# When the value operands' differences are made in the queries' sweep of a transformer block

## The chip, the cores and the metric

The kernel runs on one core of a Trainium2 chip. A core has a matrix engine (TensorE, PE), a vector engine (VectorE, DVE), a scalar engine (ScalarE, ACT), a general engine (GpSimd, POOL), and a queue that issues transfers (SyncE, SP). Each of them works through its own list of instructions in order, and they wait for each other by semaphores. SBUF is the on-chip memory; PSUM holds matrix results. The metric is the time of one execution on the device in microseconds (us), smaller being better.

## The reference

One pre-norm transformer block in float32, on x of 2048 tokens by 1024 features. The attention is among the 32 heads of one token, not among tokens; the feed-forward weights are first rounded to a table of 16 values (NF4) in blocks of 64.

```
h = layernorm(x)
q, k, v = h @ wq.T + bq, h @ wk.T + bk, h @ wv.T + bv      # as (token, 32 heads, 32)
scores = einsum('bshd,bstd->bsht', q, k) / sqrt(32)
x = x + einsum('bsht,bstd->bshd', softmax(scores), v)
h = layernorm(x)
gate, up = h @ dq1.T, h @ dq2.T                            # dq = nf4(w), 2752 wide
x = x + (silu(gate) * up) @ dq3.T
```

## The kernel before, in words

**Three sweeps and the feed-forward.** The queries', the keys' and the values' projections are three sweeps over the tokens, each in eight iterations of one pair of 128-token tiles (`NP` = 8). Then come the two feed-forward products. Every projection of a pair is a 2 x 2 block product by Strassen's scheme in Winograd's form: seven products instead of eight. `products` (L373) runs them; each product is eight matmuls on PE of 128 x 128 by 512 (`mm4`, four instructions of the program, two passes each in the trace), into the PSUM tiles z, q, r and y. ACT copies intermediate sums out of PSUM (g0, s7, u2, u4) and DVE adds the results to ce and co. After the second product and after each one behind it `products` calls `fill(n)`, where the caller puts other work: n = 7, 6, 2, 5, 3 and 4 in this order.

**The operands of a pair.** The seven products need the four quarters of the normed, transposed tokens, A11, A12, A21, A22, and four sums and differences of them, S1 to S4. The class `Inputs` (L501) makes them in the queries' sweep for all three sweeps:
- `normed_x` (L496) norms both x tiles into xn: statistics and the final step on DVE, the inverse deviation rs on POOL.
- `transposes(j)` (L513) transposes xn tile j on PE, four quarters into one PSUM tile pt, two pt per call. ACT copies each pt twice: into the operands A of the queries and keys (L520), and with the columns in another order into the operands V of the values (L522). The quarter A21 goes to tiles of its own, A21 and V21.
- `finished` (L528) lets DVE make the four differences of A (L420, L421, L422, L425), and stores A to opD of the pair in DRAM for the keys' sweep.
- `finished_v` (L532) does the same four for V and stores it to opV for the values' sweep.

pt has three buffers (`ps_t`, L475). A has two. V (tag AV), A21 and V21 have one buffer each, so a new pair's copy into AV waits until the differences of the pair before are made and its store to opV has landed.

**One iteration p of the queries' sweep** (L597): the loads of the next two x tiles are issued and their norms written down; the seven products of pair p run; at `fill(5)`, between the fifth and the sixth product, PE transposes pair p+1. After the products come the differences of A of pair p+1 (`nxt.finished`), the transposes of the queries' result and their stores to qD (`qk_T`), then `now.finished_v`, the differences of V of pair p, and a chunk of the differences of the weights of the keys or values (`weight_chunk`, L575: DVE steps at L582 to L585, loads cB, stores wtD).

**The background.** The feed-forward weights are rounded to the table by a generator, `background` (L242): per 128 x 1024 tile some fifteen steps, each one DVE operation (L257, L259, L261, L267) and mostly one ACT operation ahead of it (L266), and scalings in sixteen small ACT operations (L218). `advance` lets it go on a step at a time, `flush` transposes a finished weight tile.

**What sets the order.** PE's order is as written. The orders of DVE, ACT, POOL and SP are set when the program is built, by a scheduler that takes the written order as priority and places an instruction when, by its own estimate, what it needs is there. `tc.issue_after(x)` makes what is issued inside stand behind instruction x; `opened` is the last of the first weights' differences. So the place of a call in the text is not yet its place in an engine's list: in the program built, V's differences of pair p (called behind the products of iteration p) begin before pair p+1's copies into AV, since these need the buffer.

Of the kernel before, what the change touches and what calls it, by code (L numbers as in the profile page):

```python
# [69 lines left out]
def preln_block_kernel(  # L70
# [133 lines left out]
    def flush(steps=3):  # L204
        for _ in range(steps):
            if pending and next(pending[0], flush) is flush:
                pending.pop(0)
# [72 lines left out]
    def advance(n):  # L280
        for _ in range(n):
            with turn():
                next(bg, None)
# [78 lines left out]
    def mm4(dst, w, xop, start, stop):  # L362
        for k in range(4):
# [7 lines left out]
            )  # L371

    def products(A, fill, used=lambda name: None, apart=None):  # L373

        def mul(dst, a, w, start, stop):
            mm4(dst, A[:, a], W[w], start, stop)
            used(w)

        def copied(nm, src):
            t = pair.tile([P, TB], FP, tag=nm, name=nm)
            marked(nc.scalar.copy(t, src))  # L383
            return t

        z = ps_pj.tile([P, TB], FP, tag="z", name="z")
        mul(z, SA11, "B11", True, False)
        g0 = copied("g0", z)
        q = ps_pj.tile([P, TB], FP, tag="q", name="q")
        mul(q, S3, "T3", True, False)  # L390
        s7 = copied("s7", q)
        fill(7)
        mul(z, S2, "T2", False, False)
        u2 = copied("u2", z)
        fill(6)
        r = bank("r")
        mul(r, SA12, "B21", True, True)
        ce = pair.tile([P, E], FP, tag="C0", name="ce")
        co = pair.tile([P, E], FP, tag="C1", name="co")
        nc.vector.tensor_tensor(ce[:, 0:512], g0, r, ALU.add)  # L400
        fill(2)
        mul(z, S1, "T1", False, apart is not None)
        u4 = copied("u4", z)
        nc.vector.tensor_tensor(co[:, 512:], u4, s7, ALU.add)
        fill(5)
        if apart is None:
            mul(z, S4, "B22", False, True)
            marked(nc.scalar.copy(ce[:, 512:], z))
        else:
            y = apart.tile([P, TB], FP, tag="y", name="y", bufs=1)  # L410
            mul(y, S4, "B22", True, True)
            nc.vector.tensor_tensor(ce[:, 512:], u4, y, ALU.add)
        fill(3)
        mul(q, SA22, "T4", False, True)
        nc.vector.tensor_tensor(co[:, 0:512], u2, q, ALU.add)
        fill(4)
        return ce, co
# [14 lines left out]
    def qk_T(t, c, b):  # L432

        nc.vector.transpose(t, c.rearrange("p (h d) -> p h d", d=D))
        nc.vector.tensor_tensor(t, t, b.unsqueeze(2).to_broadcast([P, 32, 32]), ALU.add)
# [43 lines left out]
    def load_x(i):  # L479
        xt[i] = work.tile([P, E], FP, tag="x", name="xt", bufs=2)  # L480
        for n in range(2 if i == 0 else 1):
            cols = ts(n, TB) if i == 0 else slice(None)
            load = nc.sync.dma_start(xt[i][:, cols], xf[ts(i, P), cols])
        if i == 2:
            tc.add_manual_dep(
                load.ins,
                opening["first"].name,
                mybir.DependencyInfo(
                    mybir.DependencyClass.Sync, mybir.DependencyReason.DATA
                ),  # L490
                reason="the first weights come first",
            )
# [53 lines left out]
    nxt = Inputs(0)  # L546
# [25 lines left out]
    opened = last.ins  # L572
    nc.sync.dma_start(opD[0], nxt.A)

    def weight_chunk(m, k):  # L575

        b = {}
        for nm in ("B11", "B12", "B21", "B22"):
            b[nm] = work.tile([P, TB], FP, tag=f"c{nm}", name=f"c{nm}")
            nc.sync.dma_start(b[nm], block(m, int(nm[1]) - 1, int(nm[2]) - 1)[:, k, :])  # L580
        t3 = work.tile([P, TB], FP, tag="cT3", name="cT3")
        nc.vector.tensor_tensor(t3, b["B22"], b["B12"], ALU.subtract)  # L582
        nc.vector.tensor_tensor(b["B12"], b["B12"], b["B11"], ALU.subtract)
        nc.vector.tensor_tensor(b["B22"], b["B22"], b["B12"], ALU.subtract)
        nc.vector.tensor_tensor(b["B21"], b["B21"], b["B22"], ALU.subtract)  # L585
        for n, t in ((1, b["B12"]), (2, b["B22"]), (3, t3), (4, b["B21"])):
            nc.sync.dma_start(wtD[m, n][:, k, :], t)

    def next_W(m):
        return lambda name: load_W(m, name)  # L590

    def load_A(src, p):
        t = pair.tile([P, 7, 4, P], FP, tag="A", name="A", bufs=2)
        nc.sync.dma_start(t, src[p])
        return t

    for p in range(NP):  # L597
        more = p + 1 < NP
        now = nxt
        urgent["rule"] = ("scale",) if p == 0 else ()  # L600
        if more:
            load_x(2 * p + 2)
            load_x(2 * p + 3)
            with nullcontext() if p else tc.issue_after(opened):
                nxt = Inputs(p + 1)
            if p == 0:
                with tc.issue_after(hook["normed"]):
                    nc.vector.tensor_tensor(W["T4"], W["B21"], W["T2"], ALU.subtract)

        def fill(n):  # L610
            if n in (7, 3):
                flush(1)
            if n == 5 and more:
                nxt.transposes(0)
                nxt.transposes(1)
            with nullcontext() if p else tc.issue_after(opened):
                advance({3: 3, 4: 2}.get(n, 0) if p == 0 else int(n != 5))

        cs = products(now.A, fill, (lambda name: None) if more else next_W("k"), ps_t)
        flush(1)  # L620
        if more:
            nxt.finished()
        for j in range(2):
            t = work.tile([P, 32, NH], FP, tag="qd", name="qd", bufs=2)
            qk_T(t, cs[j], qb_sb)
            nc.sync.dma_start(qD[2 * p + j], t)
        with nullcontext() if p else tc.issue_after(opened):
            now.finished_v()
        weight_chunk("kv"[p // 4], p % 4)
        advance(2)  # L630
        if p == NP - 2:
            first = load_A(opD, 0)
# [553 lines left out]
    now = Unit(*units.pop(0))  # L1186
    now.first()
    for n, (g, tbp) in enumerate(passes):
        half, sides = None, []
        while now is not None and now.tbp == tbp and now.c in g:  # L1190
# [6 lines left out]
            if g[-1] == NFULL and unit.c == NFULL - 1:  # L1197
# [5 lines left out]
                now = None  # L1203
            if units:
                now = Unit(*units.pop(0))
# [52 lines left out]
```

## Time and profile before

| | us |
|---|---|
| median of 3 runs | 2465.94 (2464.23 to 2466.81) |
| profiled execution | 2468.05 |
| its span | 2466.28 |
| PE busy | 2384.2 (97% of the span) |
| DVE busy | 2015.7 (82%) |
| ACT busy | 1514.9 (61%) |
| POOL busy | 290.0 (12%) |
| mean clock granted to PE | 0.989 |

How to read the profile's lines that follow further down. A line of the waits names the waiting engine and tile, what ended the wait, and the total time, the number of waits and the longest one. A line in order of time has start, duration, engine, source line, operation, tiles written and read, and in square brackets the idle time ahead of it and what ended it. A line of stretches has the stretch, its length, the busy time of PE, of PE's weight loads, DVE, ACT and POOL with the number of instructions, then PE's granted clock (1 is full speed), the share of the transfer engines and GB/s. L numbers are lines of the kernel.

### The profile page before, as it was taken

Reading aid. Unit: us, or ns where it says so; the run is one execution under the profiler, and the core shown is the slowest. Engines: PE = TensorE matmul, PEld = TensorE weight load, DVE = VectorE, ACT = ScalarE, POOL = GpSimd, SP = SyncE. Lnnn points to the kernel's source line nnn. Section 1 sums busy time; section 2 is a strip of 40 time slices with the busy share of each in tenths; the row PEclk is TensorE's granted clock in tenths of the full one; section 3 lists DMA queues with packets and bytes.
Section 4 is the critical chain, followed back from the end, with each engine's and each line's share of the span. In section 5 each row is a group of like instructions: output and inputs, shape, how many; then the busy total and the mean of one; then the engine's idle time right before and its main releaser. Section 6 shows DMA issues by size and latency. Waiting matters only on the chain.

```text
span 2466.3 us, 36345 instructions
## 1 busy us (share of the span) xinstructions
PE 2384.2 (97%) x14000; PEld 1114.6 (45%) x14000; DVE 2015.7 (82%) x2239; ACT 1514.9 (61%) x2819; POOL 290.0 (12%) x364
## 2 busy tenths in 40 slices
PE   8899999999998899999999999999999999999998
PEld 4444455545554344444444444444444444444433
DVE  8999888679899789898989989899898998861022
ACT  4556644134445678778787786977878778751200
POOL 1010000001001012030030301203012030020300
PEclk9999999999998999999999999999999999999999
DMA  8788643656779577485784858848588385772983
GB/s 320 279 298 351 237 161 115 230 204 224 231 247 317 192 261 164 141 177 187 280 178 141 177 172 298 171 147 182 163 294 194 125 187 160 276 167 78 179 317 113
DMA packets 179549, 513.87 MB, mean 208 GB/s; under 512 B 15984, under 2 KB 70256, under 8 KB 156976
## 3 DMA queue, kind: packets, MB, share of 16 engines
q1 hardware_dynamic: 138672, 438.08, 48.7%
q0 software_dynamic: 40704, 73.47, 18.2%
q8 instruction: 110, 1.80, 0.3%
q14 instruction: 63, 0.52, 0.1%
HBM read 283.69 MB, written 227.80 MB: 207 GB/s over the span
## 4 chain that ended last, share of the span: by engine, by line
DVE 23%; issue 21%; PE 14%; ACT 7%; DMA 3%; POOL 1%; DVEq 0%; POOLq 0%; ACTq 0%; SPq 0%
DVE r L267 15%; PE z L364 5%; DMA x1d<-acc 3%; PE z L1070 2%; ACT sg L266 2%; PE q L364 2%; ACT wn L218 2%; PE po L1151 1%; ACT r L218 1%; PE y L1070 1%; DVE r L259 1%; DVE r L261 1%; ACT acc L1083 1%; DVE am L230 1%; PE rr L364 1%
## 5 line engine op out<-in xcount | busy, mean ns | idle before, releaser
L267 DVE SCALAR_TENSOR_TENSOR r<-sg,r 128x1024 f32<-128x1024 f32 x780 | 946.8, 1214 | 84.8 <-ACT sg L266 51.6
L266 ACT ACTIVATE sg<-wn 128x1024 f32<-128x1024 f32 x780 | 815.1, 1054 | 305.9 <-DVE r L267 280.6
L1085 POOL DMA_DIRECT2D x1d<-acc x280 | 244.2, 926 | 1281.0 <-ACT acc L1083 1238.1
L364 PE MATMUL z<-xB,w 128*128 128x512 f32 x720 | 327.1, 602 | 5.9 <-ACT u L989 4.2
L364 PE MATMUL z<-xT,w 128*128 128x512 f32 x656 | 300.5, 601 | 11.7 <-ACT g L975 8.0
L364 PE MATMUL q<-xT,w 128*128 128x512 f32 x656 | 291.3, 592 | 0.0
L1070 PE MATMUL z<-w,h 128*128 128x512 f32 x496 | 230.8, 593 | 2.9 <-ACT acc L1083 2.9
L364 PEld LDWEIGHTS z<-xB,w 128*128 128x128 f32 x720 | 135.1, 193 | 170.2 <-issue 152.9
L364 PEld LDWEIGHTS z<-xT,w 128*128 128x128 f32 x656 | 123.2, 192 | 165.7 <-issue 139.5
L218 ACT ACTIVATE wn<-wn,rc 128x64 f32<-128x64 f32 x736 | 189.3, 341 | 8.9 <-DVE rc L238 8.9
L364 PEld LDWEIGHTS q<-xT,w 128*128 128x128 f32 x656 | 123.2, 190 | 148.6 <-issue 146.4
L364 PE MATMUL z<-wT,A 128*128 128x512 f32 x384 | 177.1, 604 | 0.1
L364 PE MATMUL q<-wT,A 128*128 128x512 f32 x384 | 172.8, 592 | 0.0
L1070 PE MATMUL y<-w,h 128*128 128x512 f32 x320 | 152.0, 596 | 3.6 <-DVE h L1048 3.1
L364 PE MATMUL z<-wB,A 128*128 128x512 f32 x320 | 148.5, 608 | 2.0 <-ACT u L383 2.0
L364 PE MATMUL rr<-xB,w 128*128 128x512 f32 x328 | 147.5, 592 | 0.0
L1070 PEld LDWEIGHTS z<-w,h 128*128 128x128 f32 x496 | 92.6, 190 | 116.9 <-issue 100.8
L218 ACT ACTIVATE r<-r,am 128x64 f32<-128x64 f32 x456 | 116.6, 344 | 16.1 <-DVE r L267 16.0
L1083 ACT COPY acc<-z 128x512 f32<-128x512 f32 x160 | 92.6, 585 | 38.0 <-PE z L1070 29.7
L364 PEld LDWEIGHTS q<-wT,A 128*128 128x128 f32 x384 | 72.1, 190 | 86.7 <-issue 84.9
L985 DVE TENSOR_TENSOR g<-g,rr 128x512 f32<-128x512 f32 x41 | 28.0, 682 | 100.7 <-PE rr L364 100.7
L137 POOL TENSOR_TENSOR rs<-mv,eps 128x1 f32<-128x1 f32 x32 | 18.0, 562 | 762.5 <-DVE mv L134 762.5
(136 smaller groups left out, 2733.6 us busy)
## 6 DMA issues: line engine op xcount, KB each, us to landing
x1d<-acc POOLq DMA_DIRECT2D x280, 256.0 KB, 6.5
wd<-wop SPq DMA_DIRECT2D x31, 2048.0 KB, 7.3
w<-wd SPq DMA_DIRECT2D x41, 1280.0 KB, 7.7
wn<-in_w_dram SPq DMA_DIRECT2D x63, 512.0 KB, 4.2
xT<-xdT SPq DMA_DIRECT2D x28, 1024.0 KB, 8.5
xB<-xdB SPq DMA_DIRECT2D x24, 1024.0 KB, 7.0
w<-wd SPq DMA_DIRECT2D x42, 512.0 KB, 4.4
w<-wd SPq DMA_DIRECT2D x10, 1536.0 KB, 7.6
```

What stands on the lines that cost most here:

```text
L218: nc.scalar.mul(dst[:, ts(n, BLOCK)], src[:, ts(n, BLOCK)], by[:, n : n + 1])
L230: nc.vector.tensor_reduce(am[:, :nb], v.rearrange("p (b e) -> p b e", e=BLOCK), AX.X, ALU.max, apply_absolute_value=True,)
L259: nc.vector.scalar_tensor_tensor(r, v, edge, r, ALU.is_lt, ALU.max)
L261: nc.vector.scalar_tensor_tensor(r, v, edge, r, ALU.is_gt, ALU.subtract)
L266: nc.scalar.activation(t, v, AF.Copy, bias=-edge * by, scale=by)
L267: nc.vector.scalar_tensor_tensor(r, t, code, r, ALU.min, ALU.max)
L364: nc.tensor.matmul(dst, w[:, k, :], xop[:, k, :], start=start and k == 0, stop=stop and k == 3, skip_group_check=True,)
L985: nc.vector.tensor_tensor(self.g0, self.g0, r, ALU.add)
L1070: nc.tensor.matmul(dst, side[n][:, ts(q, P)], w3T[g[2 * m]][:, W3[n]], start=start and m == 0, stop=stop and m == 1, skip_group_check=True,)
L1083: nc.scalar.copy(t, src)
L1085: nc.gpsimd.dma_start(x1d[8 * tbp + 2 * q + j][n], t, accum_op=ALU.add)
L1151: nc.tensor.matmul(po, hs[c][j][:, ts(q, P)], w3T[c][:, ts(n, 512)], start=(c == g[0]), stop=False, skip_group_check=True,)
```

## The change

V's differences and their store are called one iteration earlier: directly behind `nxt.finished()`, for pair p+1 in iteration p, where before they were called for pair p in iteration p, behind the queries' results. Pair 0, whose transposes stand ahead of the loop, gets its differences of V in iteration 0 at `fill(7)`, behind `opened` as before.

```diff
         def fill(n):
             if n in (7, 3):
                 flush(1)
+            if n == 7 and p == 0:
+                with tc.issue_after(opened):
+                    now.finished_v()
             if n == 5 and more:
                 nxt.transposes(0)
                 nxt.transposes(1)
...
         flush(1)
         if more:
             nxt.finished()
+            nxt.finished_v()
         for j in range(2):
             t = work.tile([P, 32, NH], FP, tag="qd", name="qd", bufs=2)
             qk_T(t, cs[j], qb_sb)
             nc.sync.dma_start(qD[2 * p + j], t)
-        with nullcontext() if p else tc.issue_after(opened):
-            now.finished_v()
         weight_chunk("kv"[p // 4], p % 4)
```

## The prediction

> **What bounds the kernel now.** I read the totals first, then the stretches, then in the queries' sweep the waits and the order of time on TensorE (PE), ScalarE (ACT) and VectorE (DVE). "0.60 apart" below means start to start; listed durations overlap a little.
>
> From the page, the stretches and the waits of the first 240 us:
>
> ```profile
> PE 2384.2 (97%) x14000; PEld 1114.6 (45%) x14000; DVE 2015.7 (82%) x2239; ACT 1514.9 (61%) x2819; POOL 290.0 (12%) x364
> ...
> 0.00:240.00 240.00, 218.57 (x606) 105.87 (x607) 221.73 (x301) 126.74 (x268) 24.64 (x52) 0.96 0.82 309
> 240.00:480.00 240.00, 235.83 (x3659) 124.03 (x3657) 193.64 (x197) 108.09 (x216) 0.00 (x0) 1.00 0.48 181
> 720.00:860.00 140.00, 120.12 (x1563) 61.25 (x1562) 119.35 (x133) 79.91 (x167) 7.92 (x12) 0.91 0.74 247
> ...
> PE pt L517 <- ACT V L522: 13.0, 7, 2.4
> PE pt L517 <- DVE xn L358: 6.9, 3, 3.1
> ```
>
> PE bounds the whole, but not the queries' sweep (to 243 us): there DVE is the busier, 221.7 of 240 us. PE's own losses there are the two waits, both at the transposes, and the clock.
>
> Order of time, PE in iterations 3 and 4 of the sweep, ACT in iteration 4, and DVE in iteration 3:
>
> ```profile
> 118.32 1.04 PE L517 MATMUL pt<-ident,xn 128*128 128x128 f32 x8
> 121.43 0.79 PE L517 MATMUL pt<-ident,xn 128*128 128x128 f32 x4 [2.07 <-DVE xn L358]
> 123.39 1.12 PE L517 MATMUL pt<-ident,xn 128*128 128x128 f32 x4 [1.17 <-ACT V L522]
> 124.30 5.76 PE L364 MATMUL y<-wB,A 128*128 128x512 f32 x8
> ...
> 150.50 1.47 PE L517 MATMUL pt<-ident,xn 128*128 128x128 f32 x12
> 154.36 0.66 PE L517 MATMUL pt<-ident,xn 128*128 128x128 f32 x4 [2.39 <-ACT V L522]
> 154.85 3.60 PE L364 MATMUL y<-wB,A 128*128 128x512 f32 x8
> ...
> 152.25 1.57 ACT L520 COPY A<-pt 128x512 f32<-128x512 f32 x3
> 153.69 0.62 ACT L522 COPY V<-pt 128x512 f32<-128x512 f32 x1
> 157.47 1.53 ACT L522 COPY AV<-pt 128x512 f32<-128x512 f32 x3
> ...
> 120.56 0.81 DVE L358 TENSOR_SCALAR xn<-xt,mv,rs 128x1024 f32<-128x1024 f32 x1 [0.71 <-POOL rs L138]
> ```
>
> There are three pt buffers. The fourth transpose group needs one back. AV has one buffer too, still held by the pair before, so ACT first makes three A copies and the V21 copy, which frees the third pt: with u4 ahead, five copies 0.48 apart. That gives a 1.33 us stall at best (iterations 0 and 5) and 2.06 to 2.39 where u4 itself started 0.7 to 1.1 late behind other ACT work. In iteration 3 the second xn is late.
>
> The clock is the other loss:
>
> ```profile
> 63.00:69.00 6.00, 6.00 (x14) 2.74 (x14) 4.74 (x7) 4.90 (x14) 0.00 (x0) 0.72 0.00 0
> 124.00:130.00 6.00, 6.00 (x12) 2.70 (x11) 3.87 (x7) 3.21 (x6) 0.00 (x0) 0.61 0.62 226
> ```
>
> After the 2.06 us gap of iteration 1 and the two gaps of iteration 3 the y and q behind them ran at 0.72 and 0.61: y took 5.13 and 5.60 us to the next product instead of 3.43, so 1.7 and 2.2 lost. Gaps of 2.28 to 2.39 in iterations 2, 4 and 6 lost nothing.
>
> **The change, part by part.**
>
> 1. *Instructions.* None is added or removed: per set, four subtractions and additions of 0.60 (2.4 us DVE), and one opV store, eight sets. PE's order and POOL's are the same in the built program. ACT's, DVE's and SP's change up to the first pair of the keys' sweep; from there all are as before.
>
> 2. *Iteration 0.* The built order still copies A, A, A21, V21, A and only then AV three times, behind opV0. Gain 0; the 1.33 stays. On DVE, AV's first subtraction takes the slot of a 1.1 us reduction ahead of xn, so DVE idles 0.48 until rs.
>
> 3. *Iterations 1 to 6, ACT.* AV is free a pair earlier, so the order is A, AV, A, AV, A21, V21, A, AV. The fourth group now waits for the first AV copy, the third copy instead of the fifth: 2 x 0.48 = 0.96 less, 0.37 where u4 is on time. New wait: that AV copy for the previous opV to land, with the other copies and PE's fourth group behind it. Landing took 5.7 to 12.4 us (median 7.3); from issue to need there are at least 12 (iteration 1), elsewhere 15 or more. So 0; at the longest 12.4, some 0.3 once.
>
> 4. *SP.* opV moves from among the loads to directly behind opD, past both qD stores (pair 1's past one). It waits for DVE's last AV operation; the qD behind it waits for a later DVE addition anyway. So nothing behind, the x and weight loads included, starts later through it. 0, bounds 0 to 0.4 (an issue, 0.33).
>
> 5. *DVE, the cover.* Each set used to spread over its iteration. Now V of pair p+1 is done before the next pair's second xn, which gates PE. Counting the built orders up to the second xn of iterations 2 and 3: the set stands 2.4 us earlier in 2; at 3 the sets are even but one 1.14 step, the 1.1 reduction and 0.85 of small rows have moved ahead, 3.1 more. As check, the sum of my start-to-start rows over before's order from xn to xn is 69.6 us plus 3.95 idle, against 73.53 in the trace.
>
> Laid out with those rows (PE's transposes due / second xn done / y starts; before in brackets):
> - it. 1: 60.16 / 60.16 / 61.6 [63.32]. Gap 0.4, so y keeps full clock: next product 3.4 earlier.
> - it. 2: 86.5 / 87.5 / 89.9 [93.41]. xn costs 1.0; ACT's u4 stands behind a step that waits for DVE, 1.4 more. Gain kept at 3.5, none added.
> - it. 3: 115.7 / 121.5. DVE reaches this xn at 120.7 (before 120.56), whatever PE does: a 5.8 us gap. The copies' wait of 1.17 is gone, y starts at 123.2 [124.30] at half clock until the next window ends (125.2 on before's grid), and the next product comes at 127.7 [129.90]: 2.2 earlier. One more half-clock window leaves 0.5. **The 3.5 us of iterations 1 and 2 are lost here.**
> - it. 4: xn in time; u4 behind sixteen small ACT scalings to 149.05; y 151.15 [154.85], 3.7 earlier.
> - it. 5: stall 0.5 for 1.33; y 177.9 [182.62], 4.7 earlier.
> - it. 6: DVE again. The second x tile's load stands on SP behind a wtD store that waits for DVE to 174.4; loads landed in 2.6 to 8.3 us, median 5.7, so 180.5 where DVE wants it at 179.1: 1.3 lost (0 to 4). Then step, ACT step, u4, A, AV: y at 206.25 without that loss, 207.5 with it [211.35], 5.1 or 3.9 earlier. The gap is 2.0 to 3.3 us; a half-clock window costs 1.7. Gaps over 2 us in the trace cost it in two iterations of five; the longer gap I give 0.65, the shorter 0.4: 3.9 - 0.65 x 1.7 = 2.8 with the load late, 5.1 - 0.4 x 1.7 = 4.4 with it on time.
>
> I take the middle of these, **3.5 us** earlier at the end of the sweep; the ends are 2.3 later (load at its latest and two windows, rival C) and 5.1 earlier.
>
> 6. *Behind the sweep* every order is the same, PE is busy 235.8 of 240, and DVE has 46 us idle, so I carry the shift to the end. Cover gone: the windows of 720 to 860 ran at 0.91, 0.18 x 140 = 25 us of half clock; gaps falling otherwise in the windows could give or take one or two of 1.7 us.
>
> Of the clock the Trainium skill (TensorE: Matmul & The Clock Gate, "HAM oscillation — how this bites in real kernels") says that PE should have no idle gap above about 3.4 us. The trace tripped at 2.06. By the page's rule the gap of iteration 6 is free and the sum would be 4 to 5 us; with the trace's it is 3.5.
>
> **The sum and its base.** The profiled execution took 2468.05 (span 2466.28, 1.8 around it), 2.1 above the median of the runs, 2465.94. Off both: profile 2464.5, median **2462.4**. A measurement here tells about 0.2%, 4.9 us, from no change.
>
> **The rivals.**
> - *B, full gain.* DVE is no bound and all seven stalls shrink: 6 x 0.96, the late u4 (0.73 + 1.1 + 1.1 + 0.95 = 3.9), xn's 2.07 and the clock's 3.9 are 15.6 at most; DVE's idle time of 18.3 in 240 us, of which some 10 is the opening, allows about 8. For: small idle gaps of 0.4 to 0.7 at rs. Against: xn of iteration 3. Time 2458; 2456 to 2461.
> - *C, slower.* The x load of iteration 6 at its longest: 8.3 us lands at 183.1, DVE 4 late, y at 210.3 after a gap of 6 us, two half-clock windows 3.4: 2.3 later than before, 2468.3. The load may take 4.3 before DVE waits; above 6.0, with two windows, the sign turns (5.1 = 1.7 + 3.4). For: one of the seventeen took 8.3, the median is 5.7. Against: the trace of before has waits for x only at the start.
> - *D, all absorbed.* Second half-clock window in iteration 3 and one in 6, or DVE's lag handed to the keys' sweep: 2465 to 2467. For: xn of iteration 3 comes at the same time in both orders. Against: iterations 4 and 5 have DVE to spare (xn 8 us early).
> - *The change does nothing* is true of iteration 0 alone; ACT's copies do change from 1 on.
>
> **How the numbers follow.** Forecast 0.53, B 0.20, C 0.10, D 0.17. Faster by over 0.2% (below 2461.0): B at 0.18 and the forecast's tail 0.13, 0.31. Slower by over 0.2% (above 2470.9): most of C's high part, where the later windows fall badly too, 0.09. Within: 0.60. The forecast's own range is 2460.5 to 2464.5. The range for all, 2457.0 to 2467.5, leaves out B's low end and C's upper half.
>
> **What would show it.** Right: in iterations 1 to 6 ACT goes A, AV, A, AV, and "pt waits for ACT V" is replaced by waits for AV, with iteration 1 and 5 at 0.4 to 0.5 us; in iteration 3 a PE gap of 5 to 6 us that ends at xn near 121.5 us, and low clock behind it; the sweep's last product ends 2 to 5 us before 242.3; the rest shifts as one. Wrong: a second xn of iteration 3 well before 120 us (then B); a DVE wait for x in iteration 6 of over 2 us or a longer sweep (C); a keys' sweep whose PE waits have grown (D).

## The result, and the profile after

The changed kernel takes 2477.93 us (median of 5 runs, 2473.82 to 2478.33) beside 2465.59 for the kernel before: 1.0043 times as long, 95% interval 1.0031 to 1.0054. It is slower by 12.3 us between the medians and by 10.6 by the ratio, where 3.5 us of gain was forecast; the measurement lies outside the range on record, 2457.0 to 2467.5. Two of the five runs took 2473.8 and 2473.9 and three 2477.9 to 2478.3; the profiled execution, 2478.13 (span 2476.3), is one of the three.

The same stretches as before, of the changed kernel (columns: stretch, length, busy time of PE, PE's weight loads, DVE, ACT and POOL, PE's clock, share of the transfer engines, GB/s):

```profile
0.00:240.00 240.00, 217.69 (x594) 105.69 (x595) 218.44 (x295) 127.11 (x273) 23.24 (x52) 0.96 0.81 303
240.00:480.00 240.00, 231.15 (x3521) 121.28 (x3520) 192.79 (x199) 104.20 (x208) 0.00 (x0) 0.98 0.46 171
```

The queries' sweep is about as busy as before (217.7 of 240 us of PE for 218.6). The loss shows in the second row: 4.7 us less PE, at a clock of 0.98 for 1.00. PE's waits in these 480 us:

```profile
PE pt L517 <- DVE xn L358: 13.4, 5, 6.5
PE pt L517 <- ACT AV L522: 5.8, 4, 3.5
PE sc L450 <- DMA ql<-qD: 4.9, 1, 4.9
...
PE pt L517 <- ACT V L522: 1.3, 1, 1.3
```

The waits for V have gone from 13.0 us to 1.3, as forecast, and those for AV are 5.8. But the waits for xn have doubled, from 6.9 to 13.4 (some 5 of either are the opening, ahead of the sweep's iterations), and there is a new one: the scores (`sc`, the first of the keys' sweep) wait for `ql`, a load of the stored queries. In order of time on PE, iterations 3 and 6 of the queries' sweep and the place of the new wait:

```profile
117.70 1.04 PE L517 MATMUL pt<-ident,xn 128*128 128x128 f32 x8
125.22 1.97 PE L517 MATMUL pt<-ident,xn 128*128 128x128 f32 x8 [6.48 <-DVE xn L358]
...
206.94 1.47 PE L517 MATMUL pt<-ident,xn 128*128 128x128 f32 x12
211.93 1.12 PE L517 MATMUL pt<-ident,xn 128*128 128x128 f32 x4 [3.51 <-ACT AV L522]
212.83 6.10 PE L364 MATMUL y<-wB,A 128*128 128x512 f32 x8
...
285.11 1.79 PE L450 MATMUL sc<-kd,ql 32*32 32x32 f32 x128 [4.94 <-DMA ql<-qD]
286.83 5.03 PE L364 MATMUL z<-wT,A 128*128 128x512 f32 x8
```

Before, the same two instructions of the keys' sweep ran without a gap and at full clock:

```profile
276.37 1.77 PE L450 MATMUL sc<-kd,ql 32*32 32x32 f32 x128
278.07 3.70 PE L364 MATMUL z<-wT,A 128*128 128x512 f32 x8
```

So 4.94 us of wait and 5.03 - 3.70 = 1.33 of half clock arise at one place. What `ql` stood behind is seen on SP, first before, then after:

```profile
249.99 2.05 SPq L587 DMA_DIRECT2D wtDv<-cB  x2
252.09 1.24 SPq L587 DMA_DIRECT2D wtDv<-cT  x1
253.37 1.27 SPq L587 DMA_DIRECT2D wtDv<-cB  x1
254.68 1.25 SPq L594 DMA_DIRECT2D A<-opD  x1
257.81 0.84 SPq L691 DMA_DIRECT2D ql<-qD  x2
```

```profile
249.81 3.18 SPq L630 DMA_DIRECT2D qD<-qd  x2
253.04 1.18 SPq L580 DMA_DIRECT2D cB<-in_wvT_dram  x2
254.28 0.80 SPq L594 DMA_DIRECT2D A<-opD  x1
272.37 0.33 SPq L587 DMA_DIRECT2D wtDv<-cB  x1
272.75 0.42 SPq L587 DMA_DIRECT2D wtDv<-cT  x1
274.11 1.52 SPq L587 DMA_DIRECT2D wtDv<-cB  x2
275.72 0.38 SPq L594 DMA_DIRECT2D A<-opD  x1
276.16 1.59 SPq L693 DMA_DIRECT2D ql<-qD  x3
```

Two loads of the last weight chunk (`cB`, in fact cB21 and cB22) stand in the changed program behind the seven loads of the keys' weights, which wait for PE, and behind the last two stores to qD. They are issued at 253.04. So DVE makes the chunk's steps L582 to L585 among the keys' sweep's own work, where the kernel before had finished them in the queries' sweep. The last step before, then the first and the last after:

```profile
229.21 0.69 DVE L585 TENSOR_TENSOR cB<-cB,cB 128x512 f32<-128x512 f32 x1
```

```profile
269.93 0.69 DVE L582 TENSOR_TENSOR cT<-cB,cB 128x512 f32<-128x512 f32 x1
...
274.60 0.68 DVE L585 TENSOR_TENSOR cB<-cB,cB 128x512 f32<-128x512 f32 x1
```

The four wtDv stores wait for DVE on SP (17.2 us ahead of the first), and the `ql` loads behind them are issued at 276.16 where they were issued at 257.81. Not all of this is the transfer: these transfers landed at most 7.3 us after their issue, so the two loads were there by 261.3, and DVE, without a gap, came to the first step 8.6 us later. The place of the steps in DVE's list adds to the place of the loads in SP's.

How far each point of PE's list of products is behind the kernel before, from the starts of the same product in the two profiled executions (us; the runs are introduced below; the time given is that of the kernel before):

| kernel | 229: behind the last transposes | 266: keys, pair 0 | 296: behind the first scores | 432 | end |
|---|---|---|---|---|---|
| changed | +4.0 | +3.7 | +10.1 | +11.8 | +10.0 |
| a1_pool | +2.5 | +2.2 | +8.7 | +10.2 | +7.9 |
| a8_load2 | +1.7 | +1.2 | +1.2 | +2.8 | +1.6 |
| b1_late | +1.4 | +1.4 | +11.0 | +12.4 | +6.9 |
| b8_load2 | +1.7 | +1.4 | +1.4 | +1.3 | +0.5 |
| b3_move | -8.1 | -10.0 | -5.6 | +0.4 | -3.7 |
| a3n_move | -2.4 | -3.4 | -2.3 | +3.4 | +5.7 |
| c16_even | -5.8 | +0.8 | +8.6 | +8.8 | +8.6 |

Of the changed kernel's first +4.0, 1.1 are there before any changed instruction runs (the first x landed later in that execution). A gap of two microseconds costs half clock in one execution and not in another, too (behind the 2.06 us gap of iteration 1, y lost 1.7 us in the kernel before and nothing in b8_load2): single profiles of one order differ by 1 to 2 us at the end of the sweep.

### The profile page after: what moved, and what is told of

It is laid out like the page before. It is cut to its first block, busy times and chain, and to the rows that moved or that the text cites. A ratio compares the mean times of both kernels' runs of the same rounds, so it can differ in the third digit from the quotient of the medians.

```text
span 2476.3 us, 36360 instructions
## 1 busy us (share of the span) xinstructions
PE 2389.1 (96%) x14000; PEld 1117.4 (45%) x14000; DVE 2016.6 (81%) x2239; ACT 1511.3 (61%) x2819; POOL 288.5 (12%) x364
## 4 chain that ended last, share of the span: by engine, by line
DVE 28%; issue 18%; PE 12%; ACT 7%; DMA 2%; POOL 1%; DVEq 0%; POOLq 0%; ACTq 0%; SPq 0%
DVE r L267 18%; PE z L364 5%; ACT sg L266 2%; DMA x1d<-acc 2%; ACT wn L218 2%; PE q L364 2%; ACT r L218 1%; PE z L1072 1%; DVE r L259 1%; DVE r L261 1%; PE po L1153 1%; DVE am L230 1%; ACT acc L1085 1%; PE rr L364 1%; PE po L1164 1%
## 5 line engine op out<-in xcount | busy, mean ns | idle before, releaser
L267 DVE SCALAR_TENSOR_TENSOR r<-sg,r 128x1024 f32<-128x1024 f32 x780 | 946.5, 1214 | 83.1 <-ACT sg L266 47.5
L137 POOL TENSOR_TENSOR rs<-mv,eps 128x1 f32<-128x1 f32 x32 | 17.5, 546 | 776.0 <-DVE mv L134 759.3
```

The costliest lines, as they stand in the source:

```text
L267: nc.vector.scalar_tensor_tensor(r, t, code, r, ALU.min, ALU.max)
```

## The experiments

Theory 1: the late chunk and what it does to SP make the loss. Theory 2: the queries' sweep has lost the time itself, through DVE (late xn) or ACT, and the wait for ql only takes slack. Times are compared as ratios to the kernel before on the same chip.

**a1_pool: the stores off SP.**

```diff
-            nc.sync.dma_start(wtD[m, n][:, k, :], t)
+            (nc.gpsimd if (m, k) == ("v", 3) else nc.sync).dma_start(wtD[m, n][:, k, :], t)
```

> The changed kernel, with one edit: the four stores wtDv of the last weight chunk are issued on POOL's queue and not on SP's. The orders of PE and DVE stay the same. On SP the loads of ql, which stood behind these stores, come right behind the load of opD of the second pair. Theory 1 (SP's queue): the wait of PE's first scores for ql (4.94 us) and the half clock behind it (z 5.03 instead of 3.70 us, 1.33) go, and nothing takes their place: 6.3 us off 2477.9, so 2471.6, bounds 2469 to 2473.5; in the trace no PE wait for ql, and PE's first scores some 2 to 4 us later than in the kernel before (276.4) instead of 8.7. Theory 2 (the queries' sweep has lost the time, and the ql wait only took slack that a later wait takes as well): within 2 us of the changed kernel, 2476 to 2480, with another wait of about 5 us in the keys' sweep.

Measured 2474.59, ratio 1.0035 (1.0023 to 1.0047), between the two ranges expected. The wait did not go:

```profile
271.80 0.33 SPq L594 DMA_DIRECT2D A<-opD  x1
272.18 1.94 SPq L693 DMA_DIRECT2D ql<-qD  x3
```

```profile
SPq L594 <- PE q L364: 17.6, 1, 17.6
```

With the stores gone, `ql` stands behind the load of A of pair 2, which waits 17.6 us for PE to free a buffer; PE waits 5.22 for ql. So the stores held ql in the changed kernel, but they are not the only thing ahead of it that waits: the built order has ql behind the load of A as well.

**b1_late: the late chunk alone, in the kernel before.** The two loads are written behind pair 7's last store to qD; the queries' sweep is left as it was.

```diff
-            nc.sync.dma_start(b[nm], block(...)[:, k, :])
+            late = (m, k) == ("v", 3) and nm in ("B21", "B22")
+            with tc.issue_after(after.ins) if late else nullcontext():
+                nc.sync.dma_start(b[nm], block(...)[:, k, :])
...
-        weight_chunk("kv"[p // 4], p % 4)
+        weight_chunk("kv"[p // 4], p % 4, stored)
```

> The kernel before, with one edit: of the last weight chunk the loads of cB21 and cB22 are written behind pair 7's last store to qD, so that the two DVE steps that need them and the wtDv stores come late on SP, ahead of the ql loads, as in the changed kernel; the queries' sweep is as before. Theory 1: this alone makes PE wait for ql at the first scores, 3 to 6 us, and 1.3 to 1.7 of half clock with it: 2470 to 2474. Theory 2: ql is late in SP's list but PE has it in time, or the time is absorbed later: 2465 to 2467.5.

Measured 2477.02, ratio 1.0042 (1.0029 to 1.0055): this one delay costs the kernel before as much as the whole change did, and more than the 2470 to 2474 expected.

```profile
286.36 1.80 PE L450 MATMUL sc<-kd,ql 32*32 32x32 f32 x128 [8.50 <-DMA ql<-qD]
```

The wait is 8.5 us, longer than expected. Here two `wn` loads are issued just ahead of ql, and ql took 12.0 us (median) from issue to landing, for 9.2 in the changed kernel. That the `wn` loads made it so was not tested.

**a8_load2: the late chunk taken out of the changed kernel.** The two loads go through POOL's queue, which has nothing ahead of them; DVE's steps and SP's stores then stand where they stood before.

```diff
-            nc.sync.dma_start(b[nm], block(...)[:, k, :])
+            (nc.gpsimd if (m, k) == ("v", 3) and nm in ("B21", "B22") else nc.sync).dma_start(b[nm], block(...)[:, k, :])
```

> The changed kernel, with one edit: of the last weight chunk the loads of cB21 and cB22 are issued on POOL's queue, where they do not stand behind the seven loads of the keys' weights. DVE's four steps on this chunk, the wtDv stores and, behind them, the ql loads then stand where they stood in the kernel before. (In the run that moved only the stores off SP the ql loads still came late, behind the load of A of pair 2, which waits for PE; so the queue position of the stores alone was not the cause.) Theory 1, the late loads of this chunk are the cause of PE's wait for ql: no wait for ql, and the time falls by it and the half clock behind it, 4.9 + 1.3 us, to 2471.6, bounds 2469 to 2473.5. Rival, the time is lost in the queries' sweep and the wait for ql takes only slack: 2475 to 2479.

Measured 2466.85, ratio 1.0003 (0.9994 to 1.0012), below the bounds expected. The changed kernel's loss is gone. No wait for ql:

```profile
253.67 0.85 SPq L594 DMA_DIRECT2D A<-opD  x1
255.25 1.59 SPq L693 DMA_DIRECT2D ql<-qD  x2
```

```profile
277.56 1.79 PE L450 MATMUL sc<-kd,ql 32*32 32x32 f32 x128
279.28 3.70 PE L364 MATMUL z<-wT,A 128*128 128x512 f32 x8
```

The two ratios differ by 0.0040, about 10 us; 6.3 of it are the wait and the half clock at this place. The profiles differ by 8.4 at the end, 2.5 of it already ahead of the keys' sweep (opening 1.1, one half-clock window more in iteration 2). Whether the remaining few microseconds of the 10 belong to the late chunk, the intervals (each about 0.1% wide on either side) do not say.

**b8_load2: the same edit in the kernel before**, as its control.

> The kernel before with the same edit that took the changed kernel back to 2466.9: the loads of cB21 and cB22 of the last weight chunk on POOL's queue. It is the control for that run. If the edit only undoes the late chunk of the changed kernel, it does nothing here, where the chunk is not late: 2464 to 2468, no wait of PE for ql. If the edit is worth something by itself, 4 us or more, this run falls to 2462 or below, and then the late chunk costs less than the 11 us between the two runs of the changed kernel.

Measured 2468.61 beside 2468.96, ratio 1.0001 (0.9992 to 1.0009). The edit alone is worth nothing, so a8_load2 shows what the late chunk cost and what the change is without it: no gain and no loss.

**b3_move and a3n_move: less background on DVE in the queries' sweep,** in both kernels.

```diff
         weight_chunk("kv"[p // 4], p % 4)
-        advance(2)
+        advance(0)
...
             parts.append(attend(2 * p + j, qd[j], t))
-        advance(2)
+        advance(4)
```

> The kernel before, with less background work on DVE in the queries' sweep: the two steps behind each weight chunk are left to the keys' sweep, where each pair makes four for two. About 16 steps of 1.14 us of DVE, 18 us in all, leave the first 240 us. It is the base of the next run. Its own effect: the waits of PE for xn (6.9 us) should go for the most part, those for V (13.0 us) stay, and the clock behind the gap of iteration 3 comes back (2.2 us): 2458 to 2464 if DVE's load made the xn waits. If DVE's load was not what made them, 2465 to 2468. The ql loads stay behind the last wtDv stores here, as they do in the next run.

> The changed kernel with the same moving of background steps to the keys' sweep. In the built order the loads of the last weight chunk are not late here, and the queries' sweep has 18 us less of DVE work. So it shows the change without the late chunk and without DVE as the bound. Theory 1 with DVE's load as the second cause: the change now gains what was forecast or more: 3 to 8 us below the run of the kernel before with the steps moved, 2452 to 2460; second xn of iteration 3 in time, waits for AV of 0.3 to 0.5 us each. Rival (the change itself loses in the sweep, whatever DVE has to do, since ACT's AV copies or the opV stores come late): not faster than that run, with waits for AV of 1.5 us or more in half of the iterations.

Measured 2464.58, ratio 0.9989 (0.9980 to 0.9997), and 2468.69, ratio 1.0009 (1.0000 to 1.0018): with the same edit in both, and no late chunk in either, the change makes the kernel 0.2% slower; the two intervals just part. In a3n_move the loads of the last chunk are not late though the change is in it (its wtDv stores are issued from 246.45), so the change alone does not force the late chunk; where the background stands matters as well. In the traces DVE has made 13 and 14 background steps (L257 to L267) fewer ahead of the second xn of iteration 3, and 10 and 7 fewer ahead of that of iteration 6; its busy time in the first 240 us stays at 220.9 and 214.0. Neither run came into its first range: b3_move lies just above 2458 to 2464, a3n_move far above 2452 to 2460. The rival that the change loses in the sweep, whatever DVE does, was nearer here. The waits of the two in the first 480 us, first of b3_move:

```profile
PE pt L517 <- ACT V L522: 6.0, 3, 2.4
...
PE pt L517 <- DVE xn L358: 3.8, 2, 2.0
PE pt L517 <- ACT AV L522: 3.7, 4, 1.7
```

```profile
PE pt L517 <- ACT AV L522: 11.0, 6, 3.3
...
PE pt L517 <- DVE xn L358: 5.0, 2, 3.0
```

Waits of up to 3.3 us for AV with xn in time: another thing was late. It is u4, ACT's copy of the fifth product, which stands on ACT ahead of the copies out of pt. In the changed kernel's iteration 6, PE ends that product at 207.1:

```profile
206.60 2.00 ACT L266 ACTIVATE sg<-wn 128x1024 f32<-128x1024 f32 x2
209.37 1.06 ACT L266 ACTIVATE sg<-wn 128x1024 f32<-128x1024 f32 x1 [0.77 <-DVE r L267]
210.33 0.57 ACT L383 COPY u<-z 128x512 f32<-128x512 f32 x1
210.80 0.59 ACT L520 COPY A<-pt 128x512 f32<-128x512 f32 x1
211.27 0.60 ACT L522 COPY AV<-pt 128x512 f32<-128x512 f32 x1
```

u4 starts 3.23 late behind three background steps, the last of which waits for DVE. Measuring in every iteration from the end of the fifth product to the start of y, less u4's lateness, gives two constants wherever xn is in time: **3.02 to 3.13 us where ACT makes three A copies first, 2.06 to 2.12 in the order A, AV, A, AV** (up to 2.50 where the transposes themselves ran at half clock). The difference is the forecast's 0.96. The sums over iterations 1 to 6:

| kernel | product's end to y | of it u4 late | of it waits for xn | half clock in y |
|---|---|---|---|---|
| before | 25.3 | 4.2 | 2.1 | 3.9 |
| changed | 26.8 | 6.9 | 8.4 | 5.3 |
| a8_load2 | 27.3 | 7.4 | 9.1 | 3.5 |
| b3_move | 19.1 | 4.7 | 0 | 1.7 |
| a3n_move | 22.3 | 9.3 | 0 | 4.6 |
| d6_before_u4 | 15.8 | 0.2 | 0 | 0 |
| c6_after_u4 | 15.2 | 0.2 | 2.2 | 0 |
| d12_before_step | 17.5 | 1.0 | 0 | 0 |
| c12_after_step | 18.8 | 1.6 | 3.9 | 0 |
| c16_even | 20.6 | 5.9 | 2.8 | 0 |
| e3_even_step | 17.6 | 1.7 | 3.0 | 0 |

Against the kernel before, the changed one saves 4.5 us through the order of the copies (five iterations of 0.96, less 0.4 at half clock in iteration 6), pays 2.7 more for u4, and 3.3 more in iteration 3 (9.1 for 5.8), where xn decides: 1.5 more in sum, as the table has it. The order of the copies does not follow from the change alone. b3_move reaches A, AV in iterations 3 to 6 without it, only because its background stands elsewhere; the scheduler then makes V's differences early by itself. So do d6_before_u4 (iterations 2, 3 and 5) and d12_before_step (3 and 5), while c6_after_u4, c12_after_step and e3_even_step copy three times A in iteration 6. The pairs below are therefore no clean comparison of the two orders.

**d6_before_u4 and c6_after_u4: u4 kept free.** In both kernels, and in c6 the two loads through POOL as in a8_load2 (the rule is taken back behind the sweep):

```diff
-        urgent["rule"] = ("scale",) if p == 0 else ()
+        urgent["rule"] = ("scale",) if p == 0 else ("scale", "step")
...
-                advance({3: 3, 4: 2}.get(n, 0) if p == 0 else int(n != 5))
+                advance({3: 3, 4: 2}.get(n, 0) if p == 0 else {3: 2, 4: 2}.get(n, 0))
...
-        advance(2)
+        advance(3)
...
+        with tc.issue_after(hook["ql", 0]) if p == 1 else nullcontext():
             nextA = load_A(opD, p + 1) if p + 1 < NP else load_A(opV, 0)
```

> The kernel before, with the background's steps kept out of the stretch of the queries' sweep in which ACT must copy u2 and u4: none is asked for at n = 7, 6 and 2, and ACT's part of a step stands behind the last urgent copy. So from iteration 2 on no background operation stands between u2 and u4 on ACT. Also the load of A of pair 2 is held behind the first ql loads. Theory: the time from the end of the fifth product to the start of y is u4's lateness + 3.1 us here (+ 2.1 with the change); it was 25.3 us in iterations 1 to 6 of the kernel before and becomes 19.5 (3.1 each, one late u4), and the half clock of iterations 1 and 3 (3.9 us) mostly goes: 2457, bounds 2454 to 2461. Rival (DVE's late xn and the clock decide, not u4): 2464 to 2468.

> The changed kernel with the same edits as the run before it, and the two loads of the last weight chunk on POOL's queue. Theory: with u4 on time, xn in time and ql not late the change gives what it does to the order of ACT's copies, 0.96 us in each of six iterations: 5.8 us less than the run before it, 2451, bounds 2448 to 2455; waits of PE for AV of 0.34 us each. Rival (the change loses by itself: DVE makes V's differences when xn is due, whatever stands on ACT): no faster than the run before it, with waits for xn of 2 us or more.

Measured 2482.23, ratio 1.0064 (1.0049 to 1.0078), and 2476.84, ratio 1.0045 (1.0032 to 1.0058): both slower than before and outside both of their ranges. u4's lateness (0.2 us in sum) and the half clock in y (0) went as expected, and the time from the product's end to y fell to 15.8 and 15.2 us; but half clock came elsewhere (the clock of the first 240 us is 0.96 and 0.97, for 0.96 before), and so did other waits, in c6:

```profile
PE sc L450 <- DVE kd L435: 7.3, 1, 7.3
PE pt L517 <- DVE xn L358: 6.9, 5, 2.5
PE ptw L178 <- ACT r L218: 6.6, 3, 5.6
```

PE waits for the scaled weight tile (ptw). That the held-back scalings make it so is not shown: the next two runs do not hold them, and PE waits longer there. In both runs the last chunk was late again (its wtDv stores at 272.5 and 270.3). In c6, of the 10.8 us from its first step to kd on DVE, its four steps take 2.4 and background operations 8.4. By the ratios c6 is 0.19% below d6, with intervals that overlap.

**d12_before_step and c12_after_step: u4 kept free, the scalings not held.** The rule is ("step",), the steps stand at {7: 1, 3: 2, 4: 2} and two behind the chunk, and all four loads of the last chunk go through POOL.

> The kernel before, with u4 kept free of the background in the queries' sweep in a way that does not hold its scalings back (in the two runs that held them PE waited for a scaled tile, 3.6 and 6.6 us, and the keys' sweep for DVE, 5 to 7 us): no steps at n = 6 and 2, ACT's part of a step behind the last urgent copy, scalings free; the four loads of the last weight chunk on POOL's queue. Base of the next run. Theory: the time from the end of the fifth product to y is u4's lateness + 3.1 us; 6 x 3.1 plus one or two late u4 (up to 3), some 21 in place of 25.3, and the half clock of up to 3.9 us: 2459 to 2464. Rival (the DVE work that is put off comes back as a wait in the keys' sweep): 2466 to 2472.

> The changed kernel with the edits of the run before it. So no late chunk and no background between u2 and u4, except for one set of scalings. Theory: u4's lateness + 2.1 us in each iteration where xn is in time, 6 x 0.96 = 5.8 us less than the run before it, bounds 3 to 7: 2453 to 2459. Rival 1 (the change only shifts the wait to xn, since DVE makes V's differences ahead of it): within 2 us of the run before it, with waits for xn of 5 us or more in sum. Rival 2 (DVE's backlog comes back in the keys' sweep): the queries' sweep ends earlier by 5 us or more than in the kernel before, the whole by less than 2.

Measured 2487.70, ratio 1.0090 (1.0077 to 1.0104), and 2483.64, ratio 1.0074 (1.0061 to 1.0088). Again both are slower than before, through waits for the scaled tile (10.3 and 7.0 us), for g in the keys' sweep (4.5 and 5.2) and, in c12, for a load of the keys' weights (4.6). So the theory that held-back scalings make PE wait for the tile, stated ahead of d12, is not borne out. Between the two the change is 4 us faster, the intervals overlapping; in the first 240 us their sums above do not differ that way (d12 reaches A, AV in two of the six iterations without the change). So this is no proof of the 5.8. Neither time came as expected, and no rival fits: c12 has waits for xn of 8.8 us, as rival 1 said, but is not within 2 us of d12, and its sweep does not end earlier than that of the kernel before, as rival 2 had it.

**c16_even and e3_even_step: DVE's background spread evenly,** in the changed kernel with all four loads through POOL. c16 has the steps at {7: 2, 4: 2} and three behind the chunk, e3 at {7: 1, 6: 1, 3: 1, 4: 2} and two behind, with the rule ("step",).

> The changed kernel with the four loads of the last weight chunk on POOL's queue, and the background's steps asked for at other places of the queries' sweep: two at n = 7, two at n = 4 and three behind the weight chunk, in place of one each at n = 7, 6, 2, 3 and 4 and two behind. In the built order DVE has 6.3 us of background operations between the second xn of iteration 2 and that of iteration 3, where the changed kernel has 14.2. Theory (DVE's backlog makes xn of iteration 3 late): the wait for xn there, 6.5 to 7.2 us, goes but for 1, and the half clock behind it, 1 us: against the run with two loads moved (2466.9) 5 to 8 us less, 2459 to 2462, if no other wait takes its place. Rival 1 (that xn is late for another reason, the statistics or rs): the wait stays above 4 us, 2465 to 2468. Rival 2 (the wait goes, but u4 comes later on ACT or PE waits for a scaled tile): 2463 to 2470, with these waits 5 us longer in sum.

> As the run before it, with steps at n = 7, 6 and 3, two at n = 4 and two behind, and ACT's part of a step behind the last urgent copy, so that one background operation, and not two or three, stands between u2 and u4 in most iterations (the scalings still may). DVE has 6.3 us of background operations ahead of the second xn of iteration 3, too. Theory: xn of iteration 3 in time, and u4 on time but for two iterations with the sixteen scalings; the sum of the times from the end of the fifth product to y, 27.3 us with two loads moved, becomes 16 to 20, and the half clock of iteration 6 goes: 2453 to 2460. Rival: PE's wait for a scaled tile (5 us and more in the runs that kept the stretch free) takes it back: 2465 to 2480.

Measured 2476.11, ratio 1.0040 (1.0027 to 1.0053), and 2478.07, ratio 1.0044 (1.0030 to 1.0058). The wait for xn in iteration 3 is gone in both (7.17 in a8_load2, none here), so it was DVE's backlog that made it; y of iteration 6 starts in c16 at 205.5 (before 211.4), and all y of the sweep run at full clock. Yet the whole is slower. In c16:

```profile
PE z L364 <- ACT u L383: 4.6, 2, 3.5
PE z L364 <- ACT g L383: 4.6, 1, 4.6
```

```profile
281.98 1.06 ACT L266 ACTIVATE sg<-wn 128x1024 f32<-128x1024 f32 x1 [0.27 <-DVE r L267]
282.94 0.57 ACT L383 COPY g<-z 128x512 f32<-128x512 f32 x1
```

The same thing as with u4, one sweep later: ACT's copy of a product stands behind background steps that wait for DVE, which has come to them late. Of what was expected of c16 rival 2 comes nearest, but with the waits moved to the keys' sweep, and the time lies above its range: -5.8 us at 229 has become +8.6 at 296. e3 is in its rival's range, though not by that rival's wait alone: PE waits 4.2 us for scaled tiles and 5.4 for g.

No version here beats the kernel before by more than 0.2%; b3_move, at 0.11% (0.03 to 0.20) less, is the lowest, and the only one below 1 with its whole interval.

## Why the prediction was wrong

- **Step 6, that behind the sweep "every order is the same" and the shift can be carried to the end, is what failed**, and with it step 4, that nothing behind opV starts later. Step 1 had said that SP's and DVE's orders change up to the first pair of the keys' sweep; step 6 dropped it and gave the late part no price. I priced what stands behind opV on SP, not the whole of SP's list up to the first ql load. There the two loads of the last chunk had moved behind loads that wait for PE. a8_load2 and b1_late settle it: take that away and the loss is gone; put it alone into the kernel before and the loss is there. It accounts for about 10 of the 15.5 us between forecast and result, 6.3 of them seen in the trace at the first scores; 3.5 of the rest are the gain that did not come. Why the scheduler places these two loads there stays open.
- **Rival C had the sign, by another mechanism.** Its chance of being above 2470.9, 0.09 of 0.10, did not follow from its own sum, 2468.3. It priced a transfer held on SP behind a wtD store that waits for DVE, but as a load of x in iteration 6. DVE did not wait for x there. The same chain, a wtD store waiting for DVE with a load behind it, came one sweep later and hit ql.
- **Step 5, the forecast's 3.5 us in the sweep:** a8_load2 has none (+1.7 at the end of the sweep, as has b8_load2 with the old order of DVE). Iterations 1, 2 and 5 have the form laid out (stalls of 0.27 and 0.34 in 1 and 5; y of iterations 1 and 2 at 61.64 and 90.02 in a8_load2 for 61.6 and 89.9). The 5.2 us between forecast and a8_load2 were lost at three places. Iteration 3 was placed right and sized too small: the second xn starts at 122.27, where the opening is as before, for 120.7 in the sum; the gap is 7.17 for 5.8, and y comes 1.7 later than laid out. In iteration 4 u4 is 1.44 late behind sixteen scalings, and y is 1.3 us earlier than before for 3.7. In iteration 6 x was in time, but u4 is 3.0 late and the gap 3.28 (3.51 in the changed kernel), at the end of the range of 2.0 to 3.3 that I gave; y is 0.85 earlier than before for 3.9 or 5.1 and then loses 2.5 to the half clock for an expected 0.7 or 1.1. The outcome is that of rival D, all absorbed, for the change without its late chunk.
- **Step 3 was right:** the 0.96 us per iteration is there, in every kernel that copies in this order. It is worth that only if u4 is no later than before: step 5 laid u4's lateness out anew for iterations 2, 4 and 6, but too small in 4 and 6. It belongs to the order of background steps on ACT and DVE, and in sum it is 6.9 us in the changed kernel and 7.4 in a8_load2, for 4.2 before.
- **Step 2** held (stall 1.32 in iteration 0).
- **The clock** cost 5.3 us in the y of the sweep where it had cost 3.9, and it is partly luck: iteration 2 had gaps of 1.66 and 0.29 in the changed kernel and lost 1.7 behind them, and 1.67 and 0.30 in a8_load2 and lost nothing. The Trainium skill (TensorE: Matmul & The Clock Gate, "Part 1: The HAM clock gate") says that the window of the clock's monitor runs freely, so that the same kernel can fall differently; these two profiles, with the same gaps to 0.01 us, agree. That page's bound of 3.4 us on gaps does not hold here: behind gaps of 1.66 and 2.06 us y lost 1.7 us. So the trace was the better guide.

## What to carry to other kernels

Where a scheduler fixes the lists, compare the whole list of each queue, not only the neighbours of the moved instruction, and up to the point where both lists agree again: here that point lay past the first loads of the next sweep, and the loss was made there. Look for a transfer that moved behind one that waits for an engine; its price is the delay of whatever stands behind its consumer. And a stall that "shrinks by a copy" is worth that only if the copies start when they did: count what stands ahead of them on their engine in the new order too.

## What the runs showed of the hardware

An operation on POOL of one element per partition (rs, L137) takes 0.19 us alone and 1.05 to 1.16 when DVE begins an L267, of 1.2 us, just ahead of it. From the changed kernel:

```profile
85.14 0.19 POOL L137 TENSOR_TENSOR rs<-mv,eps 128x1 f32<-128x1 f32 x1 [24.49 <-DVE mv L134]
...
86.84 1.17 DVE L267 SCALAR_TENSOR_TENSOR r<-sg,r 128x1024 f32<-128x1024 f32 x1
87.00 1.06 POOL L137 TENSOR_TENSOR rs<-mv,eps 128x1 f32<-128x1 f32 x1 [1.05 <-DVE mv L134]
```

L267 reads two operands in SBUF (sg and r). The Trainium skill (SBUF — State Buffer, "SBUF: two separate sides") says that such a DVE instruction and a GpSimd instruction that reads SBUF exclude each other for the whole of an instruction; the rows agree: the second rs starts 0.16 us behind L267 and ends 0.05 us after it. For xn it meant 0.71 us of DVE idle at the second xn of iterations 2 and 3, before and after, and no experiment here took it away.

The same order of PE's list can differ by 2 us from one execution to the next at the end of the queries' sweep: b8_load2 and the kernel before, with the same orders of PE and DVE, differ by 1.7, and by 6.0 to 3.9 us in the half clock behind the gaps.
